# Key lengths with tokens on partitions, and 20 key tiles of the second attention issued beside the end of the expert layer

## The chip, the cores and the metric

The kernel runs on one core of a Trainium2 chip. Its engines are TensorE (PE, matmuls; PEld its weight loads), VectorE (DVE), ScalarE (ACT), GpSimd (POOL) and SyncE (SP), which here only issues transfers. The metric is the device time in microseconds of one execution: the median of three runs before the change was 5826.44 us (5819.25 to 5837.37).

## The reference

The network has two layers over 3125 nodes with 256 features and 100000 edges. Each adds its parts to x:

- layer 0: a graph attention of two convolutions, a linear attention of depth 4, then a mixture of 16 experts of which each node uses two, and a layer norm;
- layer 1: `x + gnn(xn) + mix(xn)`, where `xn` is the layer norm of x, and then a feed-forward network on the half of the nodes with the largest router weight.

The part that matters here is layer 1's `mix`, a second-order attention with 8 heads of 32 features:

```
qn = q / max(|q|, 1e-12) * s * temperature ;  kn = k / max(|k|, 1e-12) * s      (s = 32 ** 0.25)
kv_mod[i,j,e] = sum_n kn[n,i] kn[n,j] v1[n,e] / N         (v1 = v with a column of ones)
y = 0.5 * qn qn kv_mod + s^2 * qn (kn^T v1 / N) + s^4 * sum(v1) / N
out = (y[1:] / y[0]) @ Wproj + bproj
```

The length |k| is taken for each node and head over 32 features. The sum over all nodes (the moments) must be complete before the first query.

## The kernel before

**Tiling.** Nodes are taken in 25 tiles of P = 125, in 7 groups of 4 tiles (the last has one). Most tiles on the chip have nodes on partitions. Transposed ones have features on partitions and up to 500 nodes in a row.

**Order of the work.** A framework allots memory from pools, adds the waits, and orders each engine's instructions when the program is built: program order counts as priority, but an instruction that it takes for ready can go ahead. In the profile, for example, loads of `xTg` that belong to layer 1 (L2871) run on SP amid the end of the expert layer. [...] Memory of a closed pool can be used by a later one, which then waits for the last use of what lay there. Pools stack up from one end of SBUF.

**The expert layer** (`l0_ffn_routed`, L2036). After the routing, 16 experts run one after the other with weights from pools `f_w`, `f_wk`, `f_hid`. The last part, the *combine* (from L2194), goes over the seven groups: two gathers per tile bring the experts' rows from DRAM on POOL's queue (`g`, pool `f_back`), DVE weighs and adds them into `acc` (L2201), normalizes (L2208, L2211) into `xcur`, and norms again (L103). Three tables go to DRAM per group on SP: `x` (L2214), `xtab` (L2218), and `kvtab` (L2226), the last from tile `st`. PE transposes the group (L2026), ACT copies it and stores it as `xcols` (L2220), and PE makes keys and values for the edge attention (L140, added to a bias at L2225).

**The edge stage** (`layer1`, L3216). `l1_gnn_slots` and `by_slots` (L942) go over the edges of 25 blocks of nodes. `SLOTS` lists the edge slots per block, and a block is cut into steps of up to 16 slots, 63 in all. A step gathers rows of `kvtab` on POOL (L635), PE makes the edge features (L2596 transposes, L2599), DVE adds them (L2604), multiplies by the query and reduces (L985, L989), and weighs the values (L1014, L1020). PE sums them (L1023) and ACT copies the sum (L1027).

**The units beside it.** `l1_mix_pairs` (L2842) is a generator that computes `mix`. It loads its weights and makes tables (`pair_tables`), then for each half c of the heads it goes through 25 key tiles (one yield each) and 7 query groups (6 yields each): 134 units. `Beside` calls it after each edge step, at a rate of 134/63. A key group begins with `unit_T`: load `xTg` (L2871), project (L2879), add the bias (L2884), square (L2888), sum over a head's features with a block matrix `bd` (L2890), square root (L2892), maximum (L2893), reciprocal (L2894) and scaling (L2895), all on 128 x 500. For each tile of the group there follow the values (L2912, L2921), a transpose of the scaled keys (L2924), copied and squared by ACT (L2925, L2926), the moments (L2927 to L2933), two rounds of a selection matmul and its square (L2944, L2949), and `pairs` (L2953). The selection results pass through a pool of one buffer, `q_ps`. Queries use `unit_T` too, then L3011 to L3063, and add their result to `x` in DRAM (L3007, L3064).

**The end.** `layer1` then opens pools for `x3`, loads it from `x` (L3230), adds the edge attention's result `gout` as `part` (L3235), and runs `l1_ffn`.

Of the kernel before, what the change touches and what calls it, by code (L numbers as in the profile page):

```python
# [19 lines left out]
P = 125  # L20
# [27 lines left out]
            nc.vector.memset(self.bd[b * 32 : b * 32 + 32, b * 32 : b * 32 + 32], 1.0)  # L48


def pools(k, stack, sbuf=(), psum=()):
    out = []
    for name, bufs in sbuf:
        out.append(stack.enter_context(k.tc.tile_pool(name=name, bufs=bufs)))
    for name, bufs in psum:
        out.append(stack.enter_context(k.tc.tile_pool(name=name, bufs=bufs, space=PSUM)))
    return out
# [25 lines left out]
def tok(ap):  # L83

    return ap.rearrange("(i p) d -> p i d", p=P)
# [809 lines left out]
class Beside:  # L895


    def __init__(self, units, n, m):
        self.units, self.rate, self.due = units, n / m, 0.0

    def __call__(self):
        self.due += self.rate
# [1130 lines left out]
Tabs = namedtuple("Tabs", "x rows cols kv")  # L2033


def l0_ffn_routed(k, dram, xcur, a, over, a1):  # L2036

# [11 lines left out]
        dram.tile([NG, 128, 2, 4 * P], F32, name="xcols"), dram.tile([N, 2 * D], F32, name="kvtab3"),  # L2049
    )  # L2050
    with ExitStack() as st:
        big, one, wts, wp, gp, bp, hp, pp = pools(
            k, st,
            [("f_big", 1), ("f_one", 1), ("f_w", 3), ("f_wk", 3), ("f_g", 2), ("f_back", 14), ("f_hid", 2)],
            [("f_ps", 2)],
        )
        zero = big.tile([128, 4 * D], F32, name="zero")
        nc.gpsimd.memset(zero, 0.0)
# [98 lines left out]
        for e in range(NE):  # L2157
            w1 = load_w(k, wts, a["w1"][e], "w1")
            w2 = load_w(k, wts, a["w2"][e], "w2")
            b2 = wts.tile([128, D], F32, name="b2", tag="b2")  # L2160
            nc.sync.dma_start(b2, a["b2"][e].partition_broadcast(128))
            xe = wp.tile([128, ns, D], F32, name="xe", tag="xe")
            got = nc.sync.dma_start(
                xe, xs[e * CAP : e * CAP + CAP, :].rearrange("(p i) d -> p i d", p=128)
            )
            after(k, got, sent)
            xeT = wp.tile([128, 2, CAP], F32, name="xeT", tag="xeT")
            for c in range(2):
                ps = pp.tile([128, 512], F32, name="tp", tag="tp")
                for i in range(ns):  # L2170
                    nc.tensor.transpose(
                        ps[:, i * 128 : i * 128 + 128], xe[:, i, c * 128 : c * 128 + 128], k.ident
                    )
                nc.vector.tensor_copy(xeT[:, c], ps)
            hid = hp.tile([128, 4, CAP], F32, name="hid", tag="hid")
            for j in range(4):
                ps = pp.tile([128, 512], F32, name="mm", tag="mm")
                for c in range(2):
                    nc.tensor.matmul(
                        ps, w1[:, c, j * 128 : j * 128 + 128], xeT[:, c], start=(c == 0), stop=(c == 1)  # L2180
                    )
                nc.scalar.activation(hid[:, j], ps, AF.Relu, bias=b1[:, e, j : j + 1], scale=1.0)
            ye = wp.tile([128, ns, D], F32, name="ye", tag="ye")
            for i in range(ns):
                ps = pp.tile([128, 512], F32, name="o", tag="o")
                for j in range(4):
                    nc.tensor.matmul(
                        ps[:, :D], hid[:, j, i * 128 : i * 128 + 128], w2[:, j, :],
                        start=(j == 0), stop=(j == 3),
                    )  # L2190
                nc.vector.tensor_tensor(ye[:, i], ps[:, :D], b2, op=ALU.add)
            nc.scalar.dma_start(
                ys[e * CAP : e * CAP + CAP, :].rearrange("(p i) d -> p i d", p=128), ye
            )  # L2194
        for gi, (g0, ng) in enumerate(k.groups):
            g = slice(g0, g0 + ng)
            for i in range(g0, g0 + ng):
                for r in range(2):
                    got = bp.tile([P, D], F32, name="g", tag="g")
                    gather(k, got, ys, sloti[:, r, i : i + 1])  # L2200
                    nc.vector.scalar_tensor_tensor(  # L2201
                        acc[:, i], got, mx[r][:, i : i + 1], acc[:, i], op0=ALU.mult, op1=ALU.add
                    )

            mv, rs = group_stats(k, gp, acc[:, g], ng)
            for j in range(ng):
# [7 lines left out]
            nc.sync.dma_start(tok(tabs.x)[:, g], xcur[:, g])  # L2214
# [3 lines left out]
            nc.sync.dma_start(tok(tabs.rows)[:, g], acc[:, g])  # L2218
            xT = group_T(k, gp, pp, acc[:, g], ng)
            nc.scalar.dma_start(tabs.cols[gi, :, :, : ng * P], xT[:, :, : ng * P])  # L2220
            t = gp.tile([P, 4, 2 * D], F32, name="st", tag="st")
            for j in range(ng):
                ps = pp.tile([128, 512], F32, name="mm", tag="mm")
                row_matmul(k, ps[:P], lambda c: xT[:, c, j * P : j * P + P], lambda c: wkv[:, c], None, 2)
                nc.vector.tensor_tensor(t[:, j], ps[:P], bkv, op=ALU.add)  # L2225
            nc.sync.dma_start(tok(tabs.kv)[:, g], t[:, :ng])  # L2226
    return tabs


# [605 lines left out]
def l1_mix_pools(k, st):  # L2835
    return pools(
        k, st, [("q_one", 1), ("q_wk", 2), ("q_x", 1), ("q_sq", 3), ("q_in", 2)],
        [("q_ps", 1), ("q_a", 1), ("q_b", 1)],
    )


def l1_mix_pairs(k, tabs, a, pl):  # L2842
# [31 lines left out]
    def unit_T(xT, ch, ng, scale, factor):  # L2874
# [22 lines left out]
        )  # L2897
        return x

    for c in range(2):  # L2900
        pairs = pa.tile([128, 512], F32, name="pairs", tag="pairs")
        mom = pb.tile([128, 512], F32, name="mom", tag="mom")
        for gi, (g0, ng) in enumerate(k.groups):
            xT = load_cols(gi, ng)
            kT = unit_T(xT, 2 + c, ng, 1.0, s)
            for j in range(ng):
                i = g0 + j
                first, last = i == 0, i == NT - 1
# [13 lines left out]
                    v, ps[:P, 0, :128], bv[:, c * 128 : c * 128 + 128], op=ALU.add  # L2922
                )
                nc.tensor.transpose(ps[:P, 1, :128], kT[:, tk], k.ident)  # L2924
                nc.scalar.copy(kv[:, :128], ps[:P, 1, :128])  # L2925
                nc.scalar.activation(k2, ps[:P, 1, :128], AF.Square)  # L2926
                m0 = nc.tensor.matmul(  # L2927
                    mom[:, :257], kv[:, :128], kv, start=first, stop=last, skip_group_check=True
                )
# [10 lines left out]
                for h0 in (0, 2):  # L2940
                    ps = two()
                    for b in range(2):
                        rows = slice((h0 + b) * 32, (h0 + b) * 32 + 32)
                        nc.tensor.matmul(  # L2944
                            ps[:P, b, :496], kT[rows, tk], sel[rows], start=True, stop=True,
                            tile_position=((h0 + b) * 32, 0),
                        )
                    sq = sp.tile([128, 2, 4 * P], F32, name="sq", tag="sq")
                    nc.scalar.activation(sq[:P, :, :496], ps[:P, :, :496], AF.Square)  # L2949
# [263 lines left out]

def layer1(k, dram, a, out, tabs, order, show):  # L3216
    sub = lambda pre: {s[len(pre) :]: v for s, v in a.items() if s.startswith(pre)}
    top = ExitStack()
    (wp,) = pools(k, top, [("d_w", 1)])
    weights = l1_ffn_weights(k, wp, sub("L1_ffn_"))  # L3220
    with ExitStack() as st:
        units = l1_mix_pairs(k, tabs, sub("L1_mix_"), l1_mix_pools(k, st))
        beside = Beside(units, 2 * k.NT + 12 * len(k.groups), sum(len(steps(n)) for n in SLOTS))
        gout, sent = l1_gnn_slots(k, dram, tabs, order, a["edge_attr_64"], sub("L1_gnn_"), beside)
        beside.rest()
    with top as st:
# [46 lines left out]
def fast(k, dram, a, out, over, dump):  # L3273
# [7 lines left out]
    with ExitStack() as st:  # L3281
        (keep,) = pools(k, st, [("order", 1)])
        order_of = lambda tmp, pp: node_order(
            k, dram, a["src"], a["dst"], keep, tmp, pp, over[:, 0:2]
        )
        with ExitStack() as s2:
            (xpool,) = pools(k, s2, [("xcur", 1)])
            xcur = xpool.tile([P, k.NT, D], F32, name="xcur")
            order = layer0(k, dram, a["x"], order_of, a, xcur)
            show("x1", xcur)  # L3290
            tabs = l0_ffn_routed(k, dram, xcur, sub("L0_ffn_"), over[:, 2:3], sub("L1_gnn_"))
            show("x2", xcur)
        layer1(k, dram, a, out, tabs, order, show)


def gps_kernel(tc, a, out, dump=None):
# [53 lines left out]
```

## Time and profile before

| | us |
|---|---|
| median of three runs | 5826.44 |
| the profiled execution | 5829.55 |
| its span | 5827.8 |
| last expert's last matmuls begin | 3328.3 |
| last transposes of the combine begin | 3476.8 |
| first and last L2604 begin | 3517.8, 5561.0 |
| first and last L1027 end | 3569.2, 5575.3 |

Over the span PE is busy 4671.1 us (80%), DVE 4216.7 (72%), ACT 1582.9 (27%) and POOL 2901.4 (50%). The granted PE clock averages 0.871.

In the views, a window row gives the length of a stretch and each engine's busy time in it. A group row gives line, engine, operation, tiles and shapes, then count, busy time, mean duration in ns and the idle time before, with what ended it. A matmul in 32-bit floats shows as two instructions. In a timeline a bracket is idle time of that engine before the instruction and what ended it. `SPq` and `ACTq` are instructions that issue transfers.

### The profile page before, as it was taken

What the parts mean: (1) busy time and instruction counts of PE and PEld (TensorE: products, weight loads), DVE (VectorE), ACT (ScalarE), POOL (GpSimd) and SP (SyncE); (2) the same over time, 40 slices, a digit from 0 to 9 for tenths busy, and PEclk for the clock granted to TensorE, in tenths of its full rate; (3) what the DMA queues carried; (4) which work ended last, traced back from release to release, by engine and by line L of the source; (5) the groups of instructions that cost most, each with busy time, mean ns of one, the idle gap of its engine ahead of it and who ended that gap; (6) DMA issues with size and microseconds to landing.
All of it is one profiled execution on the core that took longest, in us unless ns stands there. A gap on an engine that the chain in (4) does not pass through costs nothing. (4 is left out here: it accounts for less than half of the span.)

```text
span 5827.8 us, 50130 instructions
## 1 busy us (share of the span) xinstructions
PE 4671.1 (80%) x16621; PEld 2785.9 (48%) x16621; DVE 4216.7 (72%) x6090; ACT 1582.9 (27%) x3284; POOL 2901.4 (50%) x2945
## 2 busy tenths in 40 slices
PE   3467997799957998789858857789888888888778
PEld 1245775566535676556545523334333434333335
DVE  5188888888578888988631256668787778878847
ACT  1033233233323334333411102222222222222221
POOL 2475775577366775667541035344444444444411
PEclk8778998799978999899859977888898789989979
DMA  5266776677466776667454355444453444545410
GB/s 152 61 197 187 217 198 187 182 210 207 146 178 192 208 207 188 198 195 208 147 164 137 109 167 173 121 124 129 137 148 119 132 124 139 150 131 150 137 59 23
DMA packets 374285, 908.58 MB, mean 156 GB/s; under 512 B 94268, under 2 KB 170074, under 8 KB 373892
## 3 DMA queue, kind: packets, MB, share of 16 engines
q0 software_dynamic: 232624, 725.48, 43.1%
q1 hardware_dynamic: 137412, 168.23, 8.9%
q10 hardware_dynamic: 3982, 11.59, 0.5%
q8 instruction: 134, 2.20, 0.2%
q14 instruction: 133, 1.09, 0.1%
HBM read 813.62 MB, written 91.30 MB: 155 GB/s over the span
## 5 line engine op out<-in xcount | busy, mean ns | idle before, releaser
L635 POOL DMA_INDIRECT kv<-kvtab,slots x2499 | 2425.6, 971 | 1742.1 <-PE acc L1023 691.6
L1170 PE MATMUL cps<-kv,ident 128*128 128x256 f32 x2644 | 688.8, 415 | 64.4 <-DVE kv L1154 63.1
L2604 DVE TENSOR_TENSOR kv<-kv,e 128x1024 f32<-128x1024 f32 (+1 forms) x448 | 503.4, 1137 | 252.1 <-PE e L2599 226.1
L1170 PEld LDWEIGHTS cps<-kv,ident 128*128 128x128 f32 x2644 | 548.9, 211 | 214.3 <-DVE kv L1154 82.4
L2599 PE MATMUL e<-weT,eaT 128*128 128x512 f32 (+1 forms) x896 | 516.6, 673 | 66.4 <-ACT eaT L2598 64.7
L1114 DVE TENSOR_TENSOR kv<-kv,qa 128x1792 f32<-128x1792 f32 (+2 forms) x230 | 478.6, 2081 | 98.4 <-DMA kv<-kvtab,slots 85.5
L1117 DVE TENSOR_REDUCE al<-kv 128x28 f32<-128x1792 f32 (+2 forms) x230 | 479.4, 2084 | 7.9
L1154 DVE TENSOR_TENSOR kv<-kv,qa 128x1792 f32<-128x1792 f32 (+2 forms) x230 | 475.3, 2074 | 0.0
L1857 PE MATMUL mm<-hTm,w 128*128 128x500 f32 (+1 forms) x896 | 364.4, 551 | 30.5 <-DVE xcur L1883 21.7
L1875 PE MATMUL mm<-w,hid 128*125 128x256 f32 x1600 | 378.5, 385 | 1.8 <-ACT hid L1865 1.8
L1023 PE MATMUL acc<-kv,ident 128*128 128x256 f32 x896 | 268.3, 463 | 76.9 <-DVE kv L1020 72.0
L1875 PEld LDWEIGHTS mm<-w,hid 128*125 128x125 f32 x1600 | 296.4, 190 | 65.2 <-issue 19.6
L2599 PEld LDWEIGHTS e<-weT,eaT 128*128 128x128 f32 (+1 forms) x896 | 153.7, 207 | 286.9 <-ACT eaT L2598 146.9
L1023 PEld LDWEIGHTS acc<-kv,ident 128*128 128x128 f32 x896 | 206.7, 237 | 165.8 <-DVE kv L1020 107.9
L1857 PEld LDWEIGHTS mm<-hTm,w 128*128 128x128 f32 x896 | 162.3, 196 | 177.5 <-issue 130.9
L989 DVE TENSOR_REDUCE al<-kv 128x56 f32<-128x1792 f32 (+2 forms) x115 | 238.7, 2075 | 4.6 <-issue 3.7
L985 DVE TENSOR_TENSOR kv<-kv,qa 128x1792 f32<-128x1792 f32 (+2 forms) x115 | 238.8, 2077 | 1.3
L1014 DVE TENSOR_TENSOR kv<-kv,al 128x1792 f32<-128x1792 f32 (+2 forms) x115 | 235.0, 2080 | 0.0
L2598 ACT COPY eaT<-e 128x128 f32<-128x128 f32 (+1 forms) x448 | 109.5, 267 | 411.7 <-PE e L2596 411.2
L1547 PE MATMUL mm<-ident,xh 125*128 125x125 f32 x400 | 96.7, 336 | 136.3 <-ACT xh L1537 128.0
L140 PE MATMUL mm<-wqv,hTm 128*125 128x512 f32 x400 | 187.5, 607 | 7.4 <-DMA wqv<-in_L_mix_Wv_dram 6.3
L1865 ACT ACTIVATE hid<-mm,b 128x500 f32<-128x500 f32 (+1 forms) x224 | 133.8, 632 | 198.3 <-PE mm L1857 196.8
(414 smaller groups left out, 7693.1 us busy)
## 6 DMA issues: line engine op xcount, KB each, us to landing
kv<-kvtab,slots POOLq DMA_INDIRECT x2499, 3.7
w<-in_L_ffn_w_dram SPq DMA_DIRECT2D x32, 512.0 KB
qd<-qT SPq DMA_DIRECT2D x24, 500.0 KB
kvtab<-st SPq DMA_DIRECT2D x12, 1000.0 KB
qT<-qd SPq DMA_DIRECT2D x24, 500.0 KB
xTg<-xcols SPq DMA_DIRECT2D x24, 500.0 KB
w<-in_L_mix_W_dram SPq DMA_DIRECT2D x8, 1024.0 KB
xs<-zero SPq DMA_DIRECT2D x16, 512.0 KB
```

The costliest lines, as they stand in the source:

```text
L635: return k.nc.gpsimd.indirect_dma_start(out=out, out_offset=None, in_=table, in_offset=bass.IndirectOffsetOnAxis(ap=index, axis=0),)
L985: nc.vector.tensor_tensor(kv[:, :m, :D], kv[:, :m, :D], q.unsqueeze(1).to_broadcast([128, m, D]), op=ALU.mult,)
L989: nc.vector.tensor_reduce(al[:, b0 : b0 + m], hv(kv[:, :m, :D]), axis=AX.X, op=ALU.add)
L1023: nc.tensor.matmul(acc[:, :D], k.ident, kv[:, j, D:], start=(b0 + j == 0), stop=(kv is bufs[-1][2] and j == left[-1]),)
L1114: nc.vector.tensor_tensor(kv[:, :m, :D], kv[:, :m, :D], q.unsqueeze(1).to_broadcast([128, m, D]), op=ALU.mult)
L1117: nc.vector.tensor_reduce(t["al"][:, b0 : b0 + m], self.heads(kv[:, :m, :D]), axis=AX.X, op=ALU.add)
L1154: nc.vector.tensor_tensor(v, v, t["w"][:, b0 : b0 + m].unsqueeze(3).to_broadcast([128, m, H, D // H]), op=ALU.mult)
L1170: self.k.nc.tensor.matmul(t["acc"][:, :D], self.k.ident, kv[:, j, D:], start=(b0 + j == 0), stop=(b == len(t["subs"]) - 1 and j == left[-1]),)
L1857: nc.tensor.matmul(ps[:, :w_], W["w1"][:, c, j * 128 : j * 128 + 128], o["hT"][:, c, :w_], start=(c == 0), stop=(c == 1),)
L1875: nc.tensor.matmul(ps[:P, :D], s["hid"][:, c, j * P : j * P + P], W["w2"][:, c, :], start=(c == 0), stop=False,)
L2599: nc.tensor.matmul(e[:, :n].rearrange("p b d -> p (b d)"), eaT[r], weT[r, :n].rearrange("p b d -> p (b d)"), start=True, stop=True,)
L2604: nc.vector.tensor_tensor(t, t, e[:, :n].unsqueeze(2).to_broadcast([128, n, 2, D]), op=ALU.add)
```

## The change

The change has four parts.

1. `l0_ffn_routed` gets a function `begin`. After the last expert it closes the experts' pools and calls it: pools of the units are opened and the generator is made. From the combine's second group on, two units are issued after each group, and eight after the last: 20 of the first half's 25 key tiles. `Beside` counts the rest, so its rate in the edge stage is 114/63.
2. The units' pools are allotted from the other end of SBUF (`side="right"`), so that they can outlive the combine's. The edge stage's pools now begin where the units' had begun. The combine has its own pools now: 12 gather buffers instead of 14, three `st` buffers instead of two, and its own PSUM pool.
3. Keys use `keys_T` instead of `unit_T`. The projected keys are not scaled. Their squares are the stationary operand, four columns of `bd` the moving one, so that a node's four lengths come out with nodes on partitions, as 16 columns per group. Root, maximum and reciprocal are taken on those.
4. Per tile, the transposed keys are scaled by DVE with the lengths spread over 32 columns (ACT copied them before), and their squares are taken from that. The selection matmuls work on unscaled keys. The length enters as the scale of the square, so each round has two squares of 496 columns, one per head, instead of one of 992.

```diff
-def pools(k, stack, sbuf=(), psum=()):
+def pools(k, stack, sbuf=(), psum=(), **where):
...
 class Beside:
     def __init__(self, units, n, m):
-        self.units, self.rate, self.due = units, n / m, 0.0
+        self.units, self.n, self.m, self.due = units, n, m, 0.0
+        self.rate = n / m
+    def ahead(self, n):
+        for _ in range(n):
+            next(self.units)
+        self.n -= n
+        self.rate = self.n / self.m
...
-        big, one, wts, wp, gp, bp, hp, pp = pools(
-            k, st,
-            [("f_big", 1), ("f_one", 1), ("f_w", 3), ("f_wk", 3), ("f_g", 2), ("f_back", 14), ("f_hid", 2)],
-            [("f_ps", 2)],
+        big, one, gp = pools(k, st, [("f_big", 1), ("f_one", 1), ("f_g", 2)])
+        ex = ExitStack()
+        wts, wp, hp, pp = pools(
+            k, ex, [("f_w", 3), ("f_wk", 3), ("f_hid", 2)], [("f_ps", 2)]
         )
...
+        ex.close()
+        fill = begin(tabs)
+        bp, sp, pp = pools(k, st, [("f_back", 12), ("f_st", 3)], [("f_ps2", 2)])
         for gi, (g0, ng) in enumerate(k.groups):
...
-            t = gp.tile([P, 4, 2 * D], F32, name="st", tag="st")
+            t = sp.tile([P, 4, 2 * D], F32, name="st", tag="st")
...
             nc.sync.dma_start(tok(tabs.kv)[:, g], t[:, :ng])
+            if gi > 0:
+                fill(2)
+        fill(8)
...
-        [("q_ps", 1), ("q_a", 1), ("q_b", 1)],
+        [("q_ps", 1), ("q_a", 1), ("q_b", 1)], side="right",
...
+    head0 = k.bd.rearrange("p (h d) -> p h d", d=32)[:, :, 0]
+
+    def keys_T(xT, ch, ng):
+        w_ = ng * P
+        ps = ps_tile()
+        for ci in range(2):
+            nc.tensor.matmul(
+                ps[:, :w_], wqkv[:, ci, ch * 128 : ch * 128 + 128],
+                xT[:, ci, :w_], start=(ci == 0), stop=(ci == 1),
+            )
+        x = wp.tile([128, 4 * P], F32, name="x", tag="x")
+        nc.scalar.activation(
+            x[:, :w_], ps[:, :w_], AF.Identity, bias=bcol[:, ch : ch + 1], scale=1.0
+        )
+        sq = xp.tile([128, 4 * P], F32, name="xsq", tag="xsq")
+        nc.scalar.activation(sq[:, :w_], x[:, :w_], AF.Square)
+        ps = ps_tile()
+        for j in range(ng):
+            nc.tensor.matmul(
+                ps[:P, j * 4 : j * 4 + 4], sq[:, j * P : j * P + P], head0, start=True, stop=True
+            )
+        r = wp.tile([P, 16], F32, name="r4", tag="r4")
+        nc.scalar.activation(r[:, : ng * 4], ps[:P, : ng * 4], AF.Sqrt)
+        nc.vector.tensor_scalar(
+            r[:, : ng * 4], r[:, : ng * 4], 1e-12, 1.0 / s, op0=ALU.max, op1=ALU.mult
+        )
+        nc.vector.reciprocal(r[:, : ng * 4], r[:, : ng * 4])
+        return x, r
...
-            kT = unit_T(xT, 2 + c, ng, 1.0, s)
+            kT, r4 = keys_T(xT, 2 + c, ng)
...
-                nc.scalar.copy(kv[:, :128], ps[:P, 1, :128])
-                nc.scalar.activation(k2, ps[:P, 1, :128], AF.Square)
+                rj = r4[:, j * 4 : j * 4 + 4]
+                nc.vector.tensor_tensor(
+                    kv[:, :128].rearrange("p (h d) -> p h d", d=32),
+                    ps[:P, 1, :128].rearrange("p (h d) -> p h d", d=32),
+                    rj.unsqueeze(2).to_broadcast([P, 4, 32]), op=ALU.mult,
+                )
+                nc.scalar.activation(k2, kv[:, :128], AF.Square)
...
-                    nc.scalar.activation(sq[:P, :, :496], ps[:P, :, :496], AF.Square)
+                    for b in range(2):
+                        nc.scalar.activation(
+                            sq[:P, b, :496], ps[:P, b, :496], AF.Square,
+                            scale=rj[:, h0 + b : h0 + b + 1],
+                        )
...
-def layer1(k, dram, a, out, tabs, order, show):
+def layer1(k, dram, a, out, tabs, order, mix):
...
-    with ExitStack() as st:
-        units = l1_mix_pairs(k, tabs, sub("L1_mix_"), l1_mix_pools(k, st))
-        beside = Beside(units, 2 * k.NT + 12 * len(k.groups), sum(len(steps(n)) for n in SLOTS))
+    beside, st = mix
+    with st:
         gout, sent = l1_gnn_slots(k, dram, tabs, order, a["edge_attr_64"], sub("L1_gnn_"), beside)
         beside.rest()
...
+            mix = ExitStack()
+            def begin(tabs):
+                units = l1_mix_pairs(k, tabs, sub("L1_mix_"), l1_mix_pools(k, mix))
+                n, m = 2 * k.NT + 12 * len(k.groups), sum(len(steps(n)) for n in SLOTS)
+                begin.beside = Beside(units, n, m)
+                return begin.beside.ahead
```

More of the change, by code (lines that the diff above doesn't have):

```diff
@@ L48, in __init__ @@
             nc.vector.memset(self.bd[b * 32 : b * 32 + 32, b * 32 : b * 32 + 32], 1.0)
-def pools(k, stack, sbuf=(), psum=()):
+def pools(k, stack, sbuf=(), psum=(), **where):
     out = []
     for name, bufs in sbuf:
-        out.append(stack.enter_context(k.tc.tile_pool(name=name, bufs=bufs)))
+        out.append(stack.enter_context(k.tc.tile_pool(name=name, bufs=bufs, **where)))
     for name, bufs in psum:
@@ L2033, with l0_ffn_routed @@
 Tabs = namedtuple("Tabs", "x rows cols kv")
-def l0_ffn_routed(k, dram, xcur, a, over, a1):
+def l0_ffn_routed(k, dram, xcur, a, over, a1, begin):
     nc, N, NT = k.nc, k.N, k.NT
@@ L3290, in fast @@
             show("x1", xcur)
-            tabs = l0_ffn_routed(k, dram, xcur, sub("L0_ffn_"), over[:, 2:3], sub("L1_gnn_"))
+            mix = ExitStack()
[4 more added lines that the diff above has]
+                return begin.beside.ahead
+            tabs = l0_ffn_routed(k, dram, xcur, sub("L0_ffn_"), over[:, 2:3], sub("L1_gnn_"), begin)
             show("x2", xcur)
-        layer1(k, dram, a, out, tabs, order, show)
+        layer1(k, dram, a, out, tabs, order, (begin.beside, mix))
 def gps_kernel(tc, a, out, dump=None):
```

## The prediction

> **What bounds the kernel now.** I began with the page, which only says that PE is busy 80% of the span and DVE 72%, and then cut the span into stages (busy time by stretch; columns: length, then busy us and instructions of PE, PE's weight loads, DVE, ACT, POOL, then granted PE clock, DMA share, GB/s).
>
> ```profile
> 3080.00:3332.00 252.00, 240.91 (x896) 160.65 (x896) 48.11 (x100) 45.26 (x65) 15.49 (x9) 0.99 0.38 128
> 3332.00:3400.00 68.00, 25.87 (x59) 12.06 (x60) 45.04 (x140) 5.14 (x12) 53.12 (x43) 0.63 0.55 162
> 3400.00:3485.00 85.00, 47.02 (x92) 18.83 (x90) 41.48 (x125) 6.07 (x16) 12.24 (x10) 0.76 0.44 155
> 3485.00:3520.00 35.00, 13.77 (x24) 5.69 (x25) 5.16 (x31) 3.59 (x11) 8.49 (x9) 0.54 0.62 196
> ```
> ```profile
> 3515.00:4007.00 492.00, 402.97 (x1339) 187.76 (x1339) 349.39 (x373) 122.74 (x278) 224.87 (x233) 0.85 0.46 134
> 4991.00:5582.00 591.00, 479.41 (x1490) 215.88 (x1486) 486.99 (x519) 135.04 (x302) 257.17 (x265) 0.90 0.46 134
> ```
>
> The expert matrices (to 3332) fill PE. In the combine (3332 to 3485) and the gap behind it PE works 86.7 of 188 us: this is the room that the change aims at. In the edge stage (3515 to 5582, both attentions together) PE is 82% busy and DVE 71 to 82%.
>
> Who waits for whom in the edge stage (columns: us in total, times, longest):
>
> ```profile
> DVE kv L2604 <- PE e L2599: 226.1, 115, 8.9
> ```
>
> DVE's largest wait is for PE, so PE's load sets the pace there. To price it I cut the stage at its 63 copies of L1027, one per step of the edge loop, and took PE's busy time of lines 2842 to 3070 (the second attention's "units") and of the other lines in each. Two steps of 14 slots show it: 41.6 us with 16.6 us of unit matmuls, 33.2 us with 6.0, so 8.4 us for 10.6. A least-squares fit over the steps gives 1.28 us per us of edge matmul and 0.90 per us of unit matmul (rms 2.4 us); fits over sums of two to four steps give 0.84 to 0.77. I use 0.85.
>
> What bounds the combine is not PE but SP's queue (timeline; start, length, instruction):
>
> ```profile
> 3431.93 4.86 SPq L2226 DMA_DIRECT2D kvtab<-st  x1
> 3436.88 4.98 SPq L2218 DMA_DIRECT2D xtab<-acc  x1
> 3441.95 7.61 SPq L2214 DMA_DIRECT2D x<-xcur  x1
> ```
>
> Such stores follow each other without a hole: from 3393.6 to 3501.7 they take 101.2 of 108.1 us. The first gathers of the edge stage need the last of them. At the end stands this (DVE's timeline):
>
> ```profile
> 3492.80 1.13 DVE L2815 COPY i<-ident 32x32 f32<-32x32 f32 x8 [15.10 <-DMA xtab<-acc]
> 3495.07 0.68 DVE L2225 TENSOR_TENSOR st<-mm,bkv 125x512 f32<-125x512 f32 x1
> ```
>
> The units' tables reuse the memory of `acc`, wait for its store, and hold up the combine's last addition.
>
> [...] 0.99 in the experts, 0.54 in the gap; units there should raise it. [...] 125-row stores of 500 KB take 4.5 to 8.8 us of SP, and the 768 KB `wqkv` load took 1.81.
>
> **The change, part by part.** Sums stand against the profiled execution, 5829.55 us (span 5827.8), 3.1 us above the median shown.
>
> *1. Twenty of 134 units leave the edge stage.* Rows of the window 3515 to 4470 (busy us, mean ns):
>
> ```profile
> L2944 PE MATMUL w<-sel,x 32*125 32x496 f32 x200 | 67.5, 734 | 4.9 <-ACT sq L2949 4.9
> L2953 PE MATMUL pairs<-sq,kvt 125*32 125x496 f32 x200 | 52.8, 659 | 8.1 <-ACT sq L2949 8.1
> L2949 ACT ACTIVATE sq<-w 125x992 f32<-125x992 f32 x50 | 49.8, 997 | 85.8 <-PE w L2944 85.8
> ```
>
> They cover 25 tiles: 2.7 + 2.1 us of PE per tile, with L2912 to L2933 (2.1) 6.9; a group's head (L2879, L2890) adds 3.1 per four tiles, so 7.7 us per unit. At 0.85 one unit is worth 6.5 us of the edge stage, all twenty 131.
>
> *2. What they cost where they go.* Alone a unit is a chain, since `q_ps` holds one buffer: value matmuls 1.06, add 0.28, transpose 0.37, scaling about 0.28, moments 1.4, two rounds of 1.3 (selection) and 1.25 (squares) of which 0.6 overlap, pairs 2.1, plus six hand-overs of about 0.2: 10.5 us, and a quarter of a 6 us head: 12 us. From about 3393 (group 1 done, weights loaded) to the first edge addition, L2604 at 3517.8, are 125 us: about 10 units fit. These are hidden behind SP's stores. The other ten run beside the first edge steps at the old price, no gain. So 10 × 6.5 = −65 us. Bounds: none hidden, 0; all, −131.
>
> *3. SP and ACT queues.* Moved ahead of the combine's stores on SP: `wqkv`, `bcol`, `bv`, `wpr`, `bpr`, and the `xTg` loads of groups 2 to 4 (those of 0 and 1 already ran there, at 3377 and 3404); on ACT's queue the eight `temp` loads (0.43 us each), past the `xcols` stores. POOL's queue gets none of them. [...] I take 15, on the path, as SP is 94% busy. The 15.1 us stall of the tables goes, as their pool no longer lies on `acc`: −6 (SP stood idle only from 3486.1 to 3491.5). The edge weights `wq`, `wsk`, `weT`, loaded at 3329 before, now lie where `xcur` was and come after it: +3 (0 to 8). DVE's in-order waits for units delay the combine's own vectors: +8 (0 to 100, see rivals). Together the edge stage starts 20 us later. Three `st` buffers instead of two take away 28 us of DVE's waits, but behind them SP is late next: 0 (down to −10). Twelve gather buffers instead of 14 still cover a group of 8: 0 (to +5).
>
> *4. Keys with tokens on partitions* (the 30 key units that stay). Each of nine heads loses DVE work:
>
> ```profile
> L2894 DVE RECIPROCAL r<-r 128x500 f32<-128x500 f32 x24 | 78.5, 3270 | 0.1
> ```
>
> 3.27 + 0.43 (L2893) + 0.67 (L2895) become a 16-column reciprocal, 0.17 by the row of L2015, and 0.2: −4.0 each, −36 us of DVE. Added: one multiply per tile, 0.28 by L2921's row, 30 × 0.28 = +8. DVE is some 0.4 of the chain of waits in this stage, so −11. PE: the `bd` matmul (1.1 us) becomes four pairs of 4-column ones, about 0.22 each pass by L2933: +0.6 × 9 = +5. The multiply is a second DVE hop before the moments; L2924 waits 35 us for the first one over 50 tiles, so 30 × 0.5 = +10, half of it hidden: +5. ACT: four squares of 496 columns for two of 992. [...] ACT is 25% busy, hidden, at most +15. Sum −1 (−15 to +20).
>
> *5. The tail.* With the units' pools at the other end, the final `x3` tile lies on the edge stage's weights and buffers instead. Now (SP, then PE):
>
> ```profile
> 5566.86 1.05 SPq L3230 DMA_DIRECT2D x<-x  x2
> 5572.45 18.37 SPq L3230 DMA_DIRECT2D x<-x  x5
> 5596.60 22.89 SPq L3235 DMA_DIRECT2D part<-gout  x7
> ```
> ```profile
> 5581.01 1.21 PE L2620 MATMUL acc<-bs,ones_row 1*128 1x256 f32 x2
> ```
>
> The loads must then wait for L2620, 5582.2 instead of 5566.9; 19.4 us of loads and 5.4 us of small ones follow, so `part` starts near 5607.5, 11 us later, and everything queued behind on SP and the last stage's first sums with it: +11 (0 to +16).
>
> Sum: −65 + 20 − 1 + 11 = −35; about 5795 profiled, 5791 as a median.
>
> **Rivals.** *All hidden:* [...] the units fit into the combine's holes, DVE's lighter heads count fully: −131 − 15 + 15 + 11 = −120, 5706. For it: PE has over 100 us of holes. Against it: 240 us of chain into 125. *A wash:* [...] each pair of units holds DVE some 24 us where the combine has 7 spare per group (period about 20 us by SP, 13 of DVE work): 6 × 10 = +60; the last eight stand before the first edge additions, 8 × 12 less the 35 us gap = +61. −131 + 121 + 11 − 1 = 0, 5826. *Slower:* the same serial wait, but the edge stage pays back only 0.6 per us of PE, because [...] DVE, already at 82% in its last part, becomes the bound: −92 + 121 + 11 = +40, 5866. It decides from a payback below 0.75. *The change does not do what it says:* the build's scheduler may put the units behind the edge work anyway, as it pulled `xTg` loads forward; then only parts 4 and 5 remain, +10, which belongs with the wash.
>
> **How the numbers follow.** Main case 0.48, its own range 5755 to 5815; all hidden 0.14; wash 0.15; slower 0.23. 0.3% (17.5 us) is about what a measurement tells from no change. Faster: 0.42 of the main case, 0.14, 0.03 of the wash: 0.59. Same: 0.06 and 0.10: 0.16. Slower: the rest, 0.25. The range 5710 to 5858 leaves out half of the fastest case and less than half of the slowest.
>
> **What would show it.** L2604's first instruction at about 3540 instead of 3517.8, with some ten tiles of selection matmuls before it; SP still full through the combine; the stage from there to the last L1027 about 65 us shorter than 2,057; key reciprocals under 0.3 us; `part` about 25 us behind the last L2620 instead of 15. Wrong if the first L2604 comes after 3590 (serial units) or the stage shrinks by less than 40 or more than 110.

## The result and the profile after

The changed kernel takes 5757.98 us (median of four runs, 5753.84 to 5764.74); the kernel before took 5822.84 beside it (5817.17 to 5837.37). The ratio is 0.9883, with a 95% interval of 0.9863 to 0.9903: 65 us less, where 35 were forecast. The profiled execution took 5757.67 us, its span is 5755.9, and the granted clock averages 0.886.

The span is cut as in the prediction: the start up to the first edge addition (L2604 before, L2619 now), the edge stage from there to the end of the last copy (L1027, now L1035), and the tail.

| us | start | edge stage | tail | span |
|---|---|---|---|---|
| before | 3517.8 | 2057.4 | 252.5 | 5827.8 |
| after | 3536.0 | 1956.3 | 263.6 | 5755.9 |
| difference | +18 | -101 | +11 | -72 |
| forecast | +20 | -66 | +11 | -35 |

Start and tail came out at the size forecast. The whole miss is in the edge stage. Windows of the changed kernel (length, then busy us and instructions of PE, its weight loads, DVE, ACT, POOL, then PE clock, DMA share, GB/s):

```profile
3332.00:3400.00 68.00, 23.07 (x57) 12.11 (x58) 33.06 (x104) 6.80 (x15) 44.80 (x36) 0.60 0.47 138
3400.00:3485.00 85.00, 77.80 (x253) 31.47 (x253) 55.68 (x179) 21.71 (x45) 17.25 (x14) 0.96 0.47 153
3485.00:3536.00 51.00, 34.99 (x100) 12.12 (x98) 3.40 (x12) 9.78 (x20) 13.43 (x15) 0.80 0.57 181
3536.00:3928.00 392.00, 348.81 (x1152) 145.31 (x1151) 264.98 (x297) 113.14 (x240) 157.48 (x165) 0.92 0.42 124
3928.00:5492.30 1564.30, 1331.05 (x4144) 601.13 (x4143) 1292.31 (x1414) 374.24 (x879) 757.62 (x768) 0.90 0.49 143
```

From 3400 to 3485 PE now works 77.8 us instead of 47.0, and its granted clock is 0.96 instead of 0.76, a rise as the prediction expected of units there. The last two rows are the first nine of the edge stage's 63 steps (steps 0 to 8) and the other 54 (9 to 62). The same two stretches of the kernel before, and both together:

```profile
3517.80:3871.10 353.30, 285.58 (x905) 133.59 (x905) 251.96 (x255) 84.34 (x191) 163.13 (x168) 0.83 0.47 135
3871.10:5575.30 1704.20, 1441.45 (x4555) 645.13 (x4555) 1345.07 (x1448) 423.00 (x930) 756.84 (x771) 0.88 0.45 134
3517.80:5575.30 2057.50, 1727.03 (x5460) 778.73 (x5460) 1597.03 (x1703) 507.34 (x1120) 919.96 (x938) 0.87 0.46 134
```

The first nine became 39 us longer, the others 140 us shorter. A second trace of the kernel before has 357.1, 1698.2 and 2055.3 us for these stretches, so differences of some 5 us between single traces mean nothing. DVE's largest wait in the edge stage (total, times, longest) fell from 226.1 us to this:

```profile
DVE kv L2619 <- PE e L2614: 172.1, 108, 9.8
```

The new key lengths cost about what their rows were forecast to (groups of the changed kernel):

```profile
L2942 DVE RECIPROCAL r<-r 125x16 f32<-125x16 f32 (+1 forms) x14 | 3.3, 236 | 0.1
L2971 DVE TENSOR_TENSOR kvt<-w,r 125x128 f32<-125x128 f32 x50 | 14.3, 285 | 9.1 <-PE w L2969 9.0
L3000 ACT ACTIVATE sq<-w,r 125x496 f32<-125x496 f32 x200 | 124.1, 669 | 191.2 <-PE w L2994 182.0 <-DMA kvtab<-st 9.1
```

The reciprocal went from 3270 to 236 ns (forecast 170). The multiply was put at 0.28 us and takes 285 ns. A square with a scale per row takes 669 ns, four of them 2.7 us per tile, where two of 992 columns took 997 ns each before (L2949).

At the tail (SP, then PE) the loads of `x3` start behind the last sum of the edges and not 14 us ahead of it, and `part` follows that sum by 29 us, where it was 16:

```profile
5495.75 22.76 SPq L3283 DMA_DIRECT2D x<-x  x7
5524.19 22.40 SPq L3288 DMA_DIRECT2D part<-gout  x7
```
```profile
5494.98 0.69 PE L2635 MATMUL acc<-bs,ones_row 1*128 1x256 f32 x2
```

### The profile page after: what moved, and what is told of

It reads as the page before. It is cut to its first block, busy times and chain, and to the rows that moved or that the text cites. A ratio compares the mean times of both kernels' runs of the same rounds, so it can differ in the third digit from the quotient of the medians.

```text
span 5755.9 us, 50336 instructions
## 1 busy us (share of the span) xinstructions
PE 4674.8 (81%) x16693; PEld 2776.6 (48%) x16693; DVE 4182.6 (73%) x6126; ACT 1586.4 (28%) x3328; POOL 2886.5 (50%) x2945
## 5 line engine op out<-in xcount | busy, mean ns | idle before, releaser
L2619 DVE TENSOR_TENSOR kv<-kv,e 128x1024 f32<-128x1024 f32 (+1 forms) x448 | 505.5, 1140 | 205.4 <-PE e L2614 172.1
L2614 PE MATMUL e<-weT,eaT 128*128 128x512 f32 (+1 forms) x896 | 498.3, 651 | 64.4 <-ACT eaT L2613 63.8
L1031 PE MATMUL acc<-kv,ident 128*128 128x256 f32 x896 | 254.2, 441 | 81.0 <-DVE kv L1028 79.5
L1031 PEld LDWEIGHTS acc<-kv,ident 128*128 128x128 f32 x896 | 193.6, 223 | 163.1 <-DVE kv L1028 108.2
L3007 PE MATMUL pairs<-sq,kvt 125*32 125x496 f32 x400 | 192.7, 624 | 17.1 <-ACT sq L3000 17.1
L3091 PE MATMUL w<-x,sel 32*128 32x500 f32 (+3 forms) x448 | 172.3, 640 | 29.2 <-ACT sq L3096 26.5
```

Of the source, the lines that this page charges most:

```text
L1031: nc.tensor.matmul(acc[:, :D], k.ident, kv[:, j, D:], start=(b0 + j == 0), stop=(kv is bufs[-1][2] and j == left[-1]),)
L2614: nc.tensor.matmul(e[:, :n].rearrange("p b d -> p (b d)"), eaT[r], weT[r, :n].rearrange("p b d -> p (b d)"), start=True, stop=True,)
L2619: nc.vector.tensor_tensor(t, t, e[:, :n].unsqueeze(2).to_broadcast([128, n, 2, D]), op=ALU.add)
```

## The experiments

Theories for the missing 35 us. A: the moved key tiles are worth more than the prediction's price, because more of them are hidden or because those left over for the first edge steps fill holes there. B: the lengths are worth more, because DVE's time counts for more than 0.4. Further ones are stated in the expectations that test them. Each ratio is to the kernel before, run beside it.

**Each half alone.** The lengths alone are the kernel before with parts 3 and 4 of the change:

```diff
-            kT = unit_T(xT, 2 + c, ng, 1.0, s)
+            kT, r4 = keys_T(xT, 2 + c, ng)
...
-                nc.scalar.copy(kv[:, :128], ps[:P, 1, :128])
+                nc.vector.tensor_tensor(... rj ... op=ALU.mult)
...
-                    nc.scalar.activation(sq[:P, :, :496], ps[:P, :, :496], AF.Square)
+                    for b in range(2):
+                        nc.scalar.activation(..., AF.Square, scale=rj[:, h0 + b : h0 + b + 1])
```

> Only the key lengths are changed, in a call of its own, as the two kernels that ran with the kernel before alone (the changed one and h1) were measured against 5823 and 5833 us. Theory A (moved units priced too low): ratio 0.998 to 1.001, edge stage 2050 to 2060 us. Theory B (lengths priced too low): ratio 0.993 to 0.996, edge stage about 30 us shorter than 2057.

Measured: 5801.03 us, 0.9949 (0.9929 to 0.9969). The opposite edit on the changed kernel leaves the tiles issued ahead and the placement, with the old lengths:

> Only the moving of 20 units with the pools at the other end, old key lengths, in a call of its own. j1, the key lengths alone, took 0.9949 of the kernel before, 30 us less. Theory B, the two halves add up: ratio 0.993 to 0.995 (about 35 us), first edge addition near 3540, edge stage about 65 us shorter, tail 11 us longer. Theory E, they need each other (short heads let the moved units run through in the combine): ratio 0.996 to 1.000, less than 70 us of unit matmuls before the first edge addition or a start later than 3555.

Measured: 5758.35 us, 0.9889 (0.9862 to 0.9915), no different from the whole change. The windows of steps 0 to 8, of steps 9 to 62 and of both, first with the lengths alone and then with the tiles ahead alone:

```profile
3524.10:3862.00 337.90, 293.52 (x941) 132.98 (x941) 238.56 (x270) 89.17 (x211) 163.16 (x168) 0.91 0.49 141
3862.00:5546.10 1684.10, 1435.66 (x4591) 635.53 (x4591) 1318.47 (x1470) 430.94 (x961) 759.27 (x771) 0.91 0.46 135
3524.10:5546.10 2022.00, 1729.17 (x5532) 768.50 (x5532) 1557.03 (x1739) 520.10 (x1170) 922.43 (x938) 0.91 0.47 136
```
```profile
3518.40:3892.10 373.70, 324.09 (x1127) 138.32 (x1124) 274.37 (x285) 110.66 (x224) 157.86 (x166) 0.91 0.44 132
3892.10:5489.00 1596.90, 1321.93 (x4105) 610.17 (x4104) 1313.25 (x1396) 368.01 (x852) 763.18 (x769) 0.88 0.47 140
3518.40:5489.00 1970.60, 1646.02 (x5231) 748.50 (x5228) 1587.62 (x1680) 478.67 (x1076) 921.04 (x934) 0.89 0.46 139
```

Set against the rows of before, either half alone does more than the forecast gave it, and they do not add:

| us | start | edge stage | tail | span |
|---|---|---|---|---|
| lengths, on the kernel before | +6 | -35 | +2 | -27 |
| then the tiles ahead | +12 | -66 | +9 | -45 |
| tiles ahead, on the kernel before | +1 | -87 | +10 | -76 |
| then the lengths | +18 | -14 | +1 | +4 |
| forecast: lengths | 0 | -1 | 0 | -1 |
| forecast: tiles ahead and placement | +20 | -65 | +11 | -34 |

So A and B are each right in size when a half stands alone. One part of the overlap can be seen in steps 0 to 8. There PE of the kernel before is idle for 67.7 of 353.3 us (285.6 busy). The lengths alone leave 44.4 us idle, the tiles alone 49.6, both 43.2: either half closes most of the same holes, and either raises the granted clock there from 0.83 to 0.91. The other part is the start, 18 us later only with both. The +6 of the lengths alone is not the change's: the last expert's last matmuls, which nothing of the change touches, already begin 7 us later in that trace (3335.5 against 3328.3).

**Eight of the twenty tiles put back.** This prices the tiles for which the forecast counted no gain.

```diff
             if gi > 0:
                 fill(2)
-        fill(8)
```

> The changed kernel without the call for eight key tiles after the combine's last group: twelve key tiles are issued beside the combine, eight go back to the edge stage, whose rate becomes 122/63. The prediction's step (only some ten key tiles are hidden, the others that are issued ahead run beside the first edge steps at the old price, no gain) expects no loss: about 5758 us, ratio to the kernel before 0.988, with the edge stage as much longer as it begins earlier. The theory that the leftover tiles get cheaper because they fill holes of the first edge steps expects 8 x (6.5 - 4.3) = 18 us more, 5775 us and 0.992, and up to 5790 us if the tiles are worth what they were with the lengths of the kernel before (8 x (6.5 - 2) = 36). First edge addition at or a few us before 3536, the tail 263 us as in the changed kernel in all cases.

Measured: 5763.86 us, 0.9895 (0.9873 to 0.9918); the intervals of this and of the whole change overlap widely. Windows of steps 0 to 8 and 9 to 62:

```profile
3530.70:3886.00 355.30, 305.53 (x1040) 135.54 (x1040) 248.22 (x282) 100.01 (x225) 153.36 (x162) 0.93 0.45 131
3886.00:5493.60 1607.60, 1373.69 (x4256) 617.34 (x4255) 1307.20 (x1429) 388.69 (x897) 760.51 (x769) 0.90 0.48 140
```

Issuing the eight tiles makes the last 54 steps 43 us shorter (1607.6 to 1564.3), the first nine 37 us longer (355.3 to 392.0) and the start 5 us later. With the new lengths they gain 3 us by the spans and 6 by the medians, close to the nothing of the forecast; the 18 us of the theory that they fill holes would be 0.9914, which the interval does not exclude. What speaks against them is that eight key tiles come before the first edge addition in both kernels (64 instructions of the selection matmuls, eight per tile): no more are hidden, and the edge stage has the same work in both.

**DVE's time put back.** To the changed kernel, one reciprocal per key head is added whose result nobody uses:

```diff
         nc.scalar.activation(sq[:, :w_], x[:, :w_], AF.Square)
+        spare = xp.tile([128, 4 * P], F32, name="r", tag="r")
+        nc.vector.reciprocal(spare[:, :w_], sq[:, :w_])
```

> The changed kernel plus, at each of the 14 heads of key groups, one reciprocal over 128 x 500 on the vector engine whose result nobody uses (the last group's is 125 wide): 3.27 us each, some ten full ones of them in the edge stage, so 33 us of that engine put back and nothing else. The forecast's weight (the vector engine is 0.4 of the chain of waits) expects 0.4 x 33 = +13, 5771 us. The theory that the lengths alone gave 33 us because vector time in the edge stage counts fully expects +33, 5791 us, and up to +7 more at the start, as the two heads in the combine hold up its additions. The theory that with the tiles issued ahead the lengths are worth nothing expects 0 to +6, 5758 to 5764 us.

Measured: 5778.85 us, 0.9913 (0.989 to 0.9935), 21 us above the changed kernel. The group, and then the window of the edge stage:

```profile
L2933 DVE RECIPROCAL r<-xsq 128x500 f32<-128x500 f32 x12 | 39.3, 3276 | 21.6 <-ACT xsq L2931 21.6
```
```profile
3528.70:5514.30 1985.60, 1691.31 (x5280) 746.00 (x5279) 1583.68 (x1718) 488.95 (x1115) 920.29 (x932) 0.90 0.46 137
```

In the edge stage DVE is busy 26.4 us longer than in the changed kernel (1583.7 against 1557.3; eight of the reciprocals fall there, not ten), and the stage is 29.3 us longer, at the same granted clock of 0.90. By these two traces DVE's time there counts about in full. PE's busy time rises by 11.5 us, though no PE work was added; even if those count at 0.85, DVE's weight is (29.3 - 9.8) / 26.4 = 0.74 and not 0.4. The whole execution says less: 35.9 us of added DVE work cost 21 us, 0.6 of it, as the edge stage begins 7 us earlier, though 10 us of that work lie before it. The intervals of the two ratios also overlap a little (from 0.989 here, up to 0.9903 for the changed kernel), so a weight above 0.4 is likely, but the times alone do not exclude 0.4.

**A version that beats both.** It keeps the whole change, and moves three pools: `x3` to the right end (the tail's wait), the edge weights' pool as well, and `f_st` ahead of the gather buffers, so that it no longer lies under the edge stage's `eat`, whose DVE instruction waits 19 us for it in the changed kernel.

```diff
-        bp, sp, pp = pools(k, st, [("f_back", 12), ("f_st", 3)], [("f_ps2", 2)])
+        sp, bp, pp = pools(k, st, [("f_st", 3), ("f_back", 12)], [("f_ps2", 2)])
...
-        (one,) = pools(k, st, [("e_one", 1)])
+        (one,) = pools(k, st, [("e_one", 1)], side="right")
...
-        xp, wp = pools(k, st, [("x3", 1), ("r_wk", 4)])
+        (xp,) = pools(k, st, [("x3", 1)], side="right")
+        (wp,) = pools(k, st, [("r_wk", 4)])
```

> The changed kernel with three placements mended: x3 at the right end (its loads no longer wait for the last edge block), the edge weights at the right end (loaded before the combine again, out of the way of the last kvtab stores), and the st buffers below the gather buffers (no DVE instruction of the edge stage waits for the last kvtab store). Against the changed kernel: tail 11 us shorter, start of the edge stage 8 to 12 us earlier, units in the gap +5: 22 to 28 us faster. Ratio to the kernel before 0.983 to 0.986 on a chip like the first, 0.996 to 0.999 on one like those of e and f.

The kernel before was run as a kernel of its own beside it:

> The kernel before, unchanged, for its profile on the chip of this call. If the chip is like those of e and f (about 6350 us), theory C says that its edge stage is no longer bound by PE: PE idle there above 450 us against 330 on the first chip, and that f0's edge stage (2339 us) is shorter than this one by 20 to 45 us, of which the start of the stage (27 us later) and the tail (11 us) take back all. Theory D says 100 us shorter. If the chip is like the first, 5820 to 5835 us.

Measured: 5733.02 us, 0.9842 (0.9811 to 0.9872); the kernel before took 5830.15, 0.9991 (0.9974 to 1.0007). SP at the tail:

```profile
5465.81 23.11 SPq L3284 DMA_DIRECT2D x<-x  x5
5500.12 23.53 SPq L3289 DMA_DIRECT2D part<-gout  x7
```

These loads start 28 us before the last sum of the edges (PE, 5493.6), and the tail takes 241.7 us, 22 less than in the changed kernel and 11 less than before. The edge stage is 13 us shorter (1943.2) and begins 12 us later (3547.6): the instruction that waited 19 us for `st` now waits 27.9 us for a gather of edge features, so that the start was not mended. The total is as expected, but not by the parts expected: the start was to come 8 to 12 us earlier.

**Runs in which the gain is gone.** In twelve runs the kernel before itself, beside them, took 6328 to 6416 us. Among them is the changed kernel again:

> The changed kernel once more, beside the two halves of the change on the same chip. In the runs of e1 to e4 the kernel before took 6346 us instead of 5823 with engines idle where the profile shows nothing that they wait for. If this chip is like the first, 5758 us against 5823 (ratio 0.988). If it is like that of e1 to e4, both theories of the chip can be told: theory C, the gain belongs to PE-bound stretches and vanishes where instructions arrive late: ratio 0.997 to 1.003; theory D, the gain is the same number of us: ratio 0.988 to 0.991.

| ratio there | first | again | again |
|---|---|---|---|
| whole change | 1.0026 (1.0009 to 1.0044) | | |
| lengths alone | 1.001 (0.999 to 1.003) | 0.9982 (0.9965 to 0.9999) | 0.9992 (0.9973 to 1.0011) |
| tiles ahead alone | 1.0002 (0.9979 to 1.0025) | 0.9998 (0.9974 to 1.0022) | 1.0006 (0.9977 to 1.0034) |
| lengths and placement, no tiles ahead | 1.003 (1.0008 to 1.0052) | 1.0005 (0.9982 to 1.0029) | 1.0041 (1.0021 to 1.006) |
| change with the spare reciprocal | 1.0049 (1.0024 to 1.0075) | 1.0066 (1.003 to 1.0101) | |

The third row is the changed kernel without its `fill` calls. What was expected of it, and of the others when they were first run:

> Only the key lengths are changed (keys_T and the scaling per tile); no unit is issued early and the pools lie as before. Theory A, the moved units were priced too low (about 8 us of edge stage each instead of 6.5): the lengths are worth what was forecast, so 5815 to 5828 us, the same as before within 0.2%. Theory B, the lengths were priced too low (DVE's freed 36 us and the shorter head count nearly in full, in the edge stage): 5785 to 5800, about 30 us faster.

> Only the moving: 20 units early, pools at the other end, but the key lengths as before (unit_T, 500-column reciprocal). Theory A: nearly all of the 65 us gained stay, 5758 to 5770. Theory B: only about half stays, 5785 to 5795, since the 20 units are worth the forecast 6.5 us each. Both: first edge addition near 3536 to 3550, end of the edge stage to the end of the kernel 11 us longer than before.

> The changed kernel without a single unit issued early: key lengths new, pools at the other end, all 134 units beside the edge steps. Against e1 it shows what the placement alone does. Forecast: the tail is 11 us longer, the stall of the tables is gone (-6), the edge weights come later (+3): 8 us slower than e1 under both theories, so 5825 to 5835 under A, 5795 to 5808 under B.

> The changed kernel with a spare 128x500 reciprocal on DVE added to each of the 14 key heads, its result unused: 14 x 3.27 = 46 us of DVE work, 9 or 10 of them in the edge stage, off the chain of the unit. Theory A: DVE counts 0.4, so +12 to +18 us against the changed kernel (5770 to 5776). Theory B: DVE counts nearly in full, +30 to +46 (5788 to 5804).

> Lengths, pools and placement of the changed kernel, but no key tile is issued beside the combine (rate 134/63 in the edge stage). The last part that has not been priced by itself is the placement, which the forecast put at +11 us (the x3 loads wait for the last sum of the edges). On top of the lengths alone (5801 us, tail 254.5 us) that gives 5812 us, ratio 0.997, with first edge addition near 3524 and the tail near 264 us. The forecast's own sum (lengths -1, tail +11) would give 5833 us, 1.002. If the placement also removes the stall of the units' tables at the combine's end (15 us on the vector engine), the first edge addition comes near 3518 and the time is 5806. The distance to the changed kernel's 5758 is then what issuing 20 key tiles ahead is worth with the new lengths: 50 us, where the forecast counted 65 less 20.

And of those that were run again:

> As e1: only the key lengths are changed. Theory A (moved units priced too low): ratio 0.998 to 1.001. Theory B (lengths priced too low): ratio 0.993 to 0.996, about 30 us faster.

> As e2: only the moving of 20 units with the pools at the other end, old key lengths. Theory A: ratio 0.988 to 0.991 (nearly all of the gain). Theory B: ratio 0.993 to 0.996 (about half of it).

> As f1, hoped to run on a chip like the first. Only the key lengths are changed. Theory A (moved units priced too low): ratio 0.998 to 1.001. Theory B (lengths priced too low): ratio 0.993 to 0.996, edge stage about 30 us shorter than 2057.

> As f2, hoped to run on a chip like the first. Only the moving, old key lengths. Theory A: ratio 0.988 to 0.991. Theory B: ratio 0.993 to 0.996, edge stage about 65 us shorter than 2057.

> As e3, hoped to run on a chip like the first: new key lengths and new places, no unit early. Theory A: ratio 0.999 to 1.003. Theory B: 0.995 to 0.998. The difference to i1 is the placement alone, forecast +8 us, of it +11 in the tail.

> As e4, hoped to run on a chip like the first: the changed kernel with a spare 128x500 reciprocal, its result unused, in each key head. Theory A: +12 to +18 us against the changed kernel (ratio 0.990 to 0.992). Theory B: +30 to +46 (0.993 to 0.997).

Nothing expected of the halves could be seen there. The spare reciprocal is the slowest of the list, though the changed kernel was not run beside it, and their intervals overlap. Theory C's range (0.997 to 1.003) holds the ratio of the whole change; its reason was not tested. The changed kernel's first edge addition came at 3807.0, its edge stage took 2338.8 us and its tail 263.3. Waits of its edge stage for nothing that the profile shows ("issue"; total, times, longest), among them:

```profile
PE e L2614 <- issue: 80.8, 56, 7.7
ACT eaT L2613 <- issue: 57.0, 29, 5.6
DVE kv L2619 <- issue: 43.8, 25, 11.6
```

In the changed kernel's first profile none of the three lines occurs: there PE has one such wait in the edge stage, of 1.5 us, and DVE and ACT have none. What holds the engines up was not found, nor whether it belongs to a chip: under the same chip number on record the kernel before took 6416 us beside one set of these runs and 5831 beside the lengths alone above. So the placement was not priced alone where the kernel before takes 5825 us. Its tail can be read here: 262.6 us with the placement and no tiles ahead, against 252.3 for the lengths alone beside it.

## Why the prediction was right or wrong

**What bounds the kernel: right in the main.** The room beside the combine was there and was used, and the edge stage follows PE's load, but not that alone (step 4).

**Step 1, the price of a unit: right.** Seventeen units fewer fall to steps 9 to 62 (54 steps, at 114/63 units each instead of 134/63). As the order of units is fixed, they are not all key tiles: by the selection matmuls, eight key tiles and two of the twelve full query groups. With the old lengths these steps became 107 us shorter, 6.3 per unit; with the new ones, against the lengths alone, 120 us, 7.0. The forecast had 6.5.

**Step 2, about ten tiles hidden, the rest at the old price: the sum was right with the new lengths, too low with the old.** Eight tiles, not ten, came before the first addition, so the edge stage holds eight key tiles less. With the new lengths it became 66 us shorter, 8.2 per hidden tile where the forecast had 6.5: two errors that cancel, which is luck. By the forecast, ten units enter steps 0 to 8 (+65) and three leave them (-19), so +46. Against the lengths alone they became 54 us longer, and the eight tiles put back agree with the zero. With the old lengths they became only 20 us longer, as PE's idle time there fell from 67.7 to 49.6 us and the clock rose from 0.83 to 0.91: that is where the 21 us come from by which the tiles ahead beat the forecast when they stand alone.

**Step 3, the start: right in size, wrong in cause.** It was priced as SP's extra loads (+15) and DVE's waits for units (+8). The tiles ahead alone issue the same loads and have no delay (+0.6; +3 counted from the last expert's last matmuls), so the 15 us for those loads, the author's estimate, did not show. Nor was SP 94% busy: the 101.2 us take in 8 idle us between the last two stores, which one row of the view joins. The 18 us come only with the lengths on top, so that the size came out is luck. `wq` and DVE's last addition of the combine, with both and then with the tiles ahead alone:

```profile
3492.02 6.85 SPq L64 DMA_DIRECT2D wq<-in_L_gnn_Wq_dram  x1
```
```profile
3499.93 0.69 DVE L2237 TENSOR_TENSOR st<-mm,bkv 125x512 f32<-125x512 f32 x1 [3.66 <-PE mm L140]
3519.76 0.21 DVE L2602 TENSOR_SCALAR eat<-base 128x1 int32<-128x1 int32 x2 [19.14 <-DMA kvtab<-st]
```
```profile
3478.46 7.19 SPq L64 DMA_DIRECT2D wq<-in_L_gnn_Wq_dram  x1
```
```profile
3484.54 0.69 DVE L2237 TENSOR_TENSOR st<-mm,bkv 125x512 f32<-125x512 f32 x1 [1.53 <-PE mm L140]
```

Both are 14 to 15 us later, and the first edge addition with them: the combine itself takes longer. A tile's longer chain (a second DVE instruction, four squares of 669 ns) is a possible cause that was only argued. Against it stands that the spare reciprocals lengthen that chain again and the start came 7 us earlier.

**Step 4, the lengths: the step that failed.** It summed to -1; alone, with all fifty tiles in the edge stage, the lengths brought 30 us (0.9949, at most 0.9969), where its prices give about nothing. Two of its terms are in doubt.

The first is the sentence "DVE is some 0.4 of the chain of waits in this stage, so −11". The amount of DVE work came out: -28 forecast, -30 measured (1587.6 to 1557.3). That is in part luck, as it was counted for 30 tiles under nine full heads, while the stage held 42 under twelve, two of them a quarter wide. But the weight is higher: 0.74 to 1.1 in the edge stage by the spare reciprocals, 0.6 over the whole execution. At 1 the step would have been -28 + 5 + 5 = -18, where -14 was measured on top of the tiles ahead; alone, DVE fell by 40 us and the stage by 35. A share of the chain of waits was read as a price. DVE is busy 71 to 82% of the stage; that a 3.3 us instruction in its queue delays the edge vectors behind it is the likely reason, but was only argued.

The second is PE's clock, which the step put at nothing. With the lengths alone the granted clock of the edge stage is 0.91 instead of 0.87, and the matmuls of the edge loop, which the lengths do not touch, are shorter (before, then the lengths alone):

```profile
L2599 PE MATMUL e<-weT,eaT 128*128 128x512 f32 x766 | 462.9, 700 | 57.7 <-ACT eaT L2598 56.1 <-DVE al L1003 0.8 <-DMA kv<-kvtab,slots 0.4
L1023 PE MATMUL acc<-kv,ident 128*128 128x256 f32 x896 | 268.3, 463 | 76.9 <-DVE kv L1020 72.0 <-issue 4.7
```
```profile
L2599 PE MATMUL e<-weT,eaT 128*128 128x512 f32 x766 | 441.7, 672 | 55.5 <-ACT eaT L2598 54.0 <-DVE al L1003 0.8 <-DMA kv<-kvtab,slots 0.4
L1023 PE MATMUL acc<-kv,ident 128*128 128x256 f32 x896 | 251.2, 440 | 86.1 <-DVE kv L1020 81.1 <-issue 4.7
```

These two groups alone are busy 38 us less, about as much as the stage gained. In these traces the clock goes roughly with PE's busy share of the stage (0.82 at 77% in the changed kernel's edge stage of 2338.8 us above, 0.87 at 84% before, 0.91 at 86% here; but 0.89 at 84% with the tiles alone), so shorter waits for DVE may themselves have raised it; no run separates the two. Only the spare reciprocals, which left the clock at 0.90, price DVE's time by itself.

How much of the 35 us each term owes depends on the order: lengths first, it is all step 4; tiles first, 13 us are step 4 and 21 us the leftover tiles. PE's busy time in the edge stage rises by 34 us when the lengths come on top (1646.0 to 1679.9), and one group shows where (tiles ahead alone, then both):

```profile
L2968 PE MATMUL pairs<-sq,kvt 125*32 125x496 f32 x336 | 91.6, 636 | 0.0
```
```profile
L3007 PE MATMUL pairs<-sq,kvt 125*32 125x496 f32 x336 | 159.5, 623 | 10.0 <-ACT sq L3000 10.0
```

Its matmuls are no longer than they were, but overlap each other less, and so cover 68 us more. That each head's matmul now waits for a square of its own is the likely reason, but was not tested.

**Step 5, the tail: right.** +11 forecast and measured, by the mechanism named; the version with three pools moved takes it away.

**The rivals.** "All hidden" was not it: eight tiles were, and its forecast (5706) lies 52 us below the result. One of its reasons seems to hold, though: DVE's lighter heads count for more than 0.4. And PE's clock rose, from 0.87 to 0.90 in the edge stage. Neither wash nor loss came: units do not stand one after the other ahead of the first edge addition, which came at 3536, not after 3590.

## What to carry to other kernels

An engine that is not the bound can pass on most of its time: DVE, busy 80% of the edge stage of the changed kernel, passed on 0.74 to 1.1 of added work there by the traces, 0.6 over the execution. Give its instructions a range of prices up to 1, and check with a spare instruction whose result is unused, which here left the clock as it was (0.90). Two changes that ease the same waits have to be tried apart and together; by the spans, the lengths cost 4 us on top of the tiles ahead where alone they had brought 27. When pools change ends, see which late load now lies on memory that is freed last: moving three pools brought another 25 us.

## What the runs showed of the hardware that was not expected

With the new lengths alone the granted PE clock in the edge stage was 0.91 instead of 0.87, though PE was busy for as long (1729.2 us against 1727.0), and a matmul of the edge features took 672 ns instead of 700.

The same program takes 5758 us in some runs and 6433 in others, where the kernel before takes 6413 and the gain is gone (1.0026). PE's granted clock in the edge stage was 0.82 there instead of 0.90, and PE, ACT and DVE stood idle for single stretches of up to 11.6 us without a recorded cause.
